# Longer minima and maxima, and other places for GpSimd's turns, in a quantile kernel

## The chip, the core and the metric

The kernel runs on one core of a Trainium2 chip. A core has TensorE (PE, matrix products into PSUM), VectorE (DVE, elementwise work), ScalarE (ACT), GpSimd (POOL) and SyncE (SP), each with its own queue of instructions, and 16 DMA engines. SBUF is the working memory of 128 partitions, PSUM holds matrix products, DRAM the large tensors. The metric is the device time of the whole program in microseconds (us), the median of several runs.

## The reference

There are 4096 nodes with 128 features. A 0/1 matrix `adj` says who is whose neighbour: each entry is 1 with probability 0.0078, so that a node has about 32 neighbours.

Layer 0 is graph attention with 8 heads: for each node a softmax over its neighbours, a weighted sum of their features, two dense products, and a layer norm. Its result is x1, again 4096 x 128.

Layer 1 takes quantiles. For each node the list of its neighbours is thinned (with more than 5 neighbours, every `skip`-th one in the list is left out, where skip is half the number, rounded up). Of the kept neighbours' rows of x1, each of the 128 features is sorted on its own, and the entries at the places of the quantiles 0.25, 0.5 and 0.75 are averaged:

```python
vals = jnp.where(keep[:, :, None], x[None, :, :], big)
svals = jnp.sort(vals, axis=1)
for q in QUANTILES:
    idx = jnp.maximum(jnp.ceil(q * n_keep).astype(jnp.int32) - 1, 0)
    picked = jnp.take_along_axis(svals, idx[:, None, None], axis=1)[:, 0, :]
    agg = agg + w_q * picked
```

The mean is mixed half and half with the node's own row, multiplied by a 128 x 128 matrix, and the own row is added.

## The kernel before

**First part (lines 302 to 494).** The kernel finds each node's neighbours from `adj`, ranks the nodes by the number of neighbours, and handles them 128 at a time, a tile, in that order: one node per partition. For the attention it fetches each neighbour's row by an indirect DMA on GpSimd's queue (`gather`, line 221; one such transfer fetches one neighbour's row for each of 128 nodes). The result x1 goes to DRAM. The lists `idx` for layer 1, and the weights `wt` that pick the quantiles, are made beside it. The change touches nothing of this.

**Second part, the quantile stage (lines 498 to 535).** Nodes are in order of their number of neighbours, so that the nodes of one tile need lists of nearly the same length. A unit is one tile, or two tiles side by side (`UNITS`, line 79): tiles 2 to 23 go in pairs, the others alone, 21 units. Their order is tile 0, tiles 24 to 31, the pairs from 22/23 down to 2/3, and tile 1.

For each unit:
- `fetch_unit` (line 509) gathers the neighbours' rows of x1 into `vals`, one slot of 128 columns for each place of the list and each tile of the unit, and the nodes' own rows into `xs`. That makes 23 to 70 gathers for one unit. `vals` has two buffers, so that a unit is fetched while another is sorted.
- `quantile_out` (line 1166) runs a selection network on VectorE: minima and maxima of slots at a distance d, stage by stage, cut down to those that the wanted places (`targets`) need. Slots that stand in a row, or at a regular step, go as one `tensor_tensor` instruction (line 1223). Results go back and forth between two buffers `work0` and `work1`, and those that are final into `goal`.
- TensorE picks the quantiles out of `goal` by products with diagonal matrices (lines 1239 to 1251), multiplies by the layer's matrix, and ScalarE copies the result `o` out of PSUM (line 1268). `write_out` (line 521) scatters `o` to the output by indirect DMAs on GpSimd's queue.

**The order on GpSimd's queue.** In the loop of lines 527 to 533 the fetch of the next unit is issued first, then the write-out of the unit that was finished before, and then the sort of the present unit goes to VectorE. So while unit k is sorted, GpSimd stands at the write-out of unit k-1, then fetches unit k+2 (into the buffer that unit k has read), then waits for unit k's result.

**Turns.** VectorE's minima and maxima and GpSimd's gathers get in each other's way. The kernel therefore puts a tiny copy from PSUM, `junk<-still` (line 1194, `turn_of_gpsimd`), into VectorE's sequence from time to time. Where it stands is decided while the program is built: `then` (line 1189) adds up an estimate `ran` of the time since the last turn, from the constants `TT_FIX`, `TT_EACH` and `TT_OVER`. Three limits use it:
- if a piece would bring `ran` above `TURN_MAX`, it is cut so that `TURN_AIM` is reached (line 1213), or, where no slot fits any more, a turn is put first (line 1215);
- after each instruction, if `ran` is above `TURN_MIN`, a turn is put (line 1230).

By that estimate 1024 columns after a turn make 0.148 + 1024 x 0.001042 = 1.215, and 2048 columns 2.282.

Of the kernel before, what the change touches and what calls it, by code (L numbers as in the profile page):

```python
# [87 lines left out]


TT_FIX, TT_EACH, TT_OVER = 0.148, 0.001042, 0.077  # L90
TURN_MIN, TURN_AIM, TURN_MAX = 1.25, 1.45, 1.7


R_NUM, R_OWN, R_F1 = L, L + 1, L + 2
# [1401 lines left out]
```

## Time and profile before

| | us |
|---|---|
| median of 3 runs (lowest, highest) | 3682.77 (3679.86, 3687.81) |
| the profiled execution, whole | 4612.32 |
| its span, first to last instruction | 4610.5 |
| first gather of `vals` | 2539.1 after the start of the span |
| VectorE busy from 2680 to 3350 | 647.8 of 670 |
| VectorE busy from 3350 to 4605 | 1047.2 of 1255 |
| GpSimd busy from 3350 to 4605 | 615.8 of 1255 |

The profiled execution is recorded by the hardware's profiler, instruction by instruction, and took 930 us longer than the runs do. Shares and sums in the profile are of that execution. In the profile a group is written as line, engine, operation, what it writes and reads, and its number; behind the bar stand busy time, mean duration in ns, and the idle time of the engine just before, with what ended it. A list in order of time has the start, the duration, and in brackets the idle time before. A GpSimd record of a gather is the making of its descriptors, and not the transfer of the data.

### The profile page before, as it was taken

To read this page: it belongs to the slowest core of one execution; us is meant where nothing else is said; L and a number is where in the kernel's file an instruction comes from. 1 tells how busy PE (TensorE), PEld (TensorE's weight loads), DVE (VectorE), ACT (ScalarE), POOL (GpSimd) and SP (SyncE) were. 2 spreads that over 40 slices of the span, in tenths; PEclk is the share of its full clock that TensorE was granted. 3 is DMA by queue.
4 is the path that set the end of the run, shared out by engine and by line. 5 is a ranking of instruction groups with operands and counts; after the bars stand their busy time and mean duration, and the time that the engine had idled before them with its cause. 6 is when DMAs were issued, how large, how long until landed. Compare 5 with 4: busy or idle time off the path is not lost. (4 is left out here: it accounts for less than half of the span.)

```text
span 4610.5 us, 23017 instructions
## 1 busy us (share of the span) xinstructions
PE 1260.0 (27%) x5372; PEld 961.7 (21%) x5375; DVE 2754.3 (60%) x7608; ACT 399.4 (9%) x555; POOL 2364.5 (51%) x2344
## 2 busy tenths in 40 slices
PE   5264546555243425334245000000000000000001
PEld 2023323333243425324245000000000000000001
DVE  6274446655142212212254289989987977887788
ACT  2020212211011001000001000000000000000000
POOL 1616543243755566464532756677665355565530
PEclk9995556555556555555555555555555555555555
DMA  5321423220211111111110111111111011111100
GB/s 186 92 90 48 141 69 101 96 94 23 61 43 38 43 43 50 36 45 45 45 29 20 50 35 39 41 44 42 41 38 34 24 32 31 36 39 37 36 22 4
DMA packets 109537, 237.71 MB, mean 52 GB/s; under 512 B 47072, under 2 KB 63456, under 8 KB 101200
## 3 DMA queue, kind: packets, MB, share of 16 engines
q0 software_dynamic: 74464, 156.55, 12.2%
q10 hardware_dynamic: 14848, 70.85, 4.5%
q1 hardware_dynamic: 20080, 8.77, 0.8%
q8 instruction: 44, 0.72, 0.1%
q14 instruction: 101, 0.83, 0.1%
HBM read 224.85 MB, written 11.15 MB: 51 GB/s over the span
## 5 line engine op out<-in xcount | busy, mean ns | idle before, releaser
L221 POOL DMA_INDIRECT G<-xt_d,idx x1127 | 1090.3, 967 | 1109.5 <-PE y L1012 696.0
L221 POOL DMA_INDIRECT vals<-x_d,idx x1024 | 1076.9, 1052 | 337.5 <-issue 302.0
L1223 DVE TENSOR_TENSOR work<-work 128x512 f32<-128x512 f32 (+6 forms) x1405 | 960.6, 712 | 35.8 <-remote 22.1
L1223 DVE TENSOR_TENSOR work<-work,work 128x512 f32<-128x512 f32 (+5 forms) x958 | 605.6, 656 | 47.6 <-remote 35.7
L1242 PE MATMUL st_ps<-dg,goal 128*128 128x128 f32 x286 | 71.8, 430 | 1935.4 <-DVE goal L1223 1791.8
L1012 PE MATMUL y<-wide,G 128*128 128x32 f32 (+2 forms) x2254 | 463.1, 381 | 97.3 <-issue 71.6
L1242 PEld LDWEIGHTS st_ps<-dg,goal 128*128 128x128 f32 x286 | 63.9, 325 | 1941.5 <-issue 1940.6
L1012 PEld LDWEIGHTS y<-wide,G 128*128 128x128 f32 x2254 | 443.6, 297 | 120.4 <-issue 86.1
L976 DVE TENSOR_SCALAR rden<-small 4x256 f32<-4x256 f32 x32 | 13.0, 407 | 648.1 <-remote 583.6
L650 DVE MAX8 first<-key 128x8 f32<-128x128 f32 x1024 | 225.5, 282 | 253.6 <-remote 128.7
L230 POOL DMA_INDIRECT out_dram<-o,own_i x32 | 50.8, 1588 | 556.6 <-ACT o L1268 539.2
L1194 DVE COPY junk<-still 128x1 f32<-128x1 f32 x1295 | 194.6, 150 | 206.2 <-remote 97.4
L683 PE MATMUL key<-sgn,markb 128*128 128x512 bf16 x256 | 147.2, 575 | 398.9 <-DVE first L650 171.2
L982 PE MATMUL rz<-rden,ownT 4*128 4x32 f32 (+6 forms) x460 | 113.3, 416 | 515.9 <-DVE rden L977 431.4
L982 PEld LDWEIGHTS rz<-rden,ownT 4*128 4x128 f32 x460 | 101.8, 317 | 532.2 <-issue 364.0
L1031 PE MATMUL hT<-late,W_sb 128*128 128x128 f32 x512 | 112.8, 409 | 238.1 <-issue 160.2
L644 ACT ACTIVATE sgn<-adj_t 128x2048 bf16<-128x2048 int32 x64 | 122.1, 1908 | 557.3 <-PE key L683 273.5
L1223 DVE TENSOR_TENSOR work<-vals 128x1024 f32<-128x1024 f32 (+8 forms) x140 | 138.7, 1007 | 32.7 <-DMA vals<-x_d,idx 32.4
L1031 PEld LDWEIGHTS hT<-late,W_sb 128*128 128x128 f32 x512 | 104.7, 312 | 249.7 <-issue 167.1
L1241 ACT ACTIVATE dg<-ident,wt 128x128 f32<-128x128 f32 x143 | 47.6, 394 | 1191.8 <-PE st_ps L1242 1191.5
L686 PE MATMUL key<-parts,oneb 64*128 64x512 bf16 x256 | 146.5, 572 | 4.8 <-issue 4.6
L1042 PE MATMUL small<-W_sb,late 128*128 128x128 f32 x512 | 120.3, 429 | 33.4 <-DVE late L1039 33.4
(184 smaller groups left out, 1743.0 us busy)
## 6 DMA issues: line engine op xcount, KB each, us to landing
adj_t<-in_adj_dram ACTq DMA_DIRECT2D x64, 1024.0 KB
G<-xt_d,idx POOLq DMA_INDIRECT x1127
vals<-x_d,idx POOLq DMA_INDIRECT x1024
R<-rec_d SPq DMA_DIRECT2D x128, 26.2 KB
xt_d<-rec SPq DMA_DIRECT2D x4, 544.0 KB
rec<-in_x_dram ACTq DMA_DIRECT2D x4, 512.0 KB
narrow<-rec_d SPq DMA_DIRECT2D x72, 5.2 KB
a_b<-in_L_gnn_a_dram ACTq DMA_DIRECT2D x2, 512.0 KB
```

The source lines that it names most:

```text
L221: nc.gpsimd.indirect_dma_start(out=dst, out_offset=None, in_=rows, in_offset=bass.IndirectOffsetOnAxis(ap=idx, axis=0),)
L644: nc.scalar.activation(sgn, adj_t, AF.Sign, accum_out=cnt[:, i : i + 1])
L650: nc.vector.max(first[:, ts(c0 // CW + c, 8)], key[:, ts(c, CW)])
L683: nc.tensor.matmul(key, lhsT=markb, rhs=sgn[:, ts(b, 512)], start=True, stop=False)
L686: nc.tensor.matmul(key, lhsT=oneb[0:64, :], rhs=parts[1][:, ts(r - 1, 512)] if r else parts[0], start=False, stop=True)
L982: nc.tensor.matmul(rz[:, layer[i] * H : (layer[i] + w - g0) * H], lhsT=ownT[w][:, r, :], rhs=rden.rearrange("p (g r h) -> p r g h", r=k // ...
L1012: nc.tensor.matmul(yf[:, ts(g, c)], lhsT=G[:, col + j - a, 0:D], rhs=pf[:, ts(j, c)], start=(i == 0 and g % (w // 2) == w // 2 - 1), stop= ...
L1031: nc.tensor.matmul(hT[:, ts(h, P)], lhsT=consts["W_sb"][:, h, :], rhs=yT[:, h, :], start=True, stop=True)
L1042: nc.tensor.matmul(o, lhsT=hv[:, h, :], rhs=consts["W1_sb"][:, h, :], start=(h == 0), stop=(h == H - 1))
L1194: nc.vector.tensor_copy(junk, late["still"])
L1223: nc.vector.tensor_tensor(slots_of(dst, (j, c, s, m), size), slots_of(a, (i, c, s, m), size), slots_of(b, (i + d, c, s, m), size), op,)
L1242: nc.tensor.matmul(st_ps[:, u, :], lhsT=goal[:, (j * k + u) * D : (j * k + u + 1) * D], rhs=dg, start=(j == 0), stop=False,)
```

## The change

Only the three limits change:

```diff
 TT_FIX, TT_EACH, TT_OVER = 0.148, 0.001042, 0.077
-TURN_MIN, TURN_AIM, TURN_MAX = 1.25, 1.45, 1.7
+TURN_MIN, TURN_AIM, TURN_MAX = 1.1, 1.9, 2.4
```

An instruction of 2048 columns (2.282 by the estimate) is now left whole where it follows a turn; before, it was cut at about 1024 to 1152 columns. An instruction of 1024 columns (1.215) is now followed by a turn at once; before, this was so only where the next piece didn't fit. What is compared with what, and in which order, stays the same, as do all instructions of the other engines.

## The prediction

> **What bounds the kernel now.** I read the page's busy times and slices first, then the groups by line, then the list in order of time around two places, then the busy times by stretch. The page splits the program at about 2540 us. Before it TensorE, GpSimd and VectorE share the attention layer. After it VectorE is busy in seven to nine tenths of every slice and TensorE almost nowhere: the quantile stage, the only one that the change touches.
>
> Groups of the page (busy us, mean ns, then idle before and what ended it):
>
> ```profile
> L221 POOL DMA_INDIRECT vals<-x_d,idx x1024 | 1076.9, 1052 | 337.5 <-issue 302.0
> ...
> L1223 DVE TENSOR_TENSOR work<-work 128x512 f32<-128x512 f32 (+6 forms) x1405 | 960.6, 712 | 35.8 <-remote 22.1
> L1223 DVE TENSOR_TENSOR work<-work,work 128x512 f32<-128x512 f32 (+5 forms) x958 | 605.6, 656 | 47.6 <-remote 35.7
> ...
> L230 POOL DMA_INDIRECT out_dram<-o,own_i x32 | 50.8, 1588 | 556.6 <-ACT o L1268 539.2
> ...
> L1194 DVE COPY junk<-still 128x1 f32<-128x1 f32 x1295 | 194.6, 150 | 206.2 <-remote 97.4
> ```
>
> GpSimd waits 539 us in this stage for a finished unit (the write-out stands in its queue behind the fetch), while VectorE waits for data only at the start. So VectorE bounds the stage and GpSimd has slack. How the two mesh shows in order of time (start, duration, engine):
>
> ```profile
> 3299.07 1.30 POOL L221 DMA_INDIRECT vals<-x_d,idx  x1 [0.30 <-issue]
> 3299.48 0.14 DVE L1194 COPY junk<-still 128x1 f32<-128x1 f32 x1
> 3299.55 1.28 DVE L1223 TENSOR_TENSOR work<-work,work 128x512 f32<-128x512 f32 x2
> 3300.68 0.97 POOL L221 DMA_INDIRECT vals<-x_d,idx  x1 [0.30 <-issue]
> 3300.75 0.14 DVE L1194 COPY junk<-still 128x1 f32<-128x1 f32 x1
> 3300.82 0.41 DVE L1223 TENSOR_TENSOR work<-work,work 128x256 f32<-128x256 f32 x1
> ```
>
> A gather takes 0.94 us when nothing is in its way (most of them do). One that starts during a run of minima and maxima lasts longer by exactly the time to the next turn: 3299.07 + 1.30 - 0.94 = 3299.43, the turn's start. Pairing the trace's lists of both engines: of some 420 lengthened gathers between 2690 and 4560 us, 262 end their wait within 0.05 us of a turn's start; most others end it where VectorE itself stood still. So: one gather per turn, and the turn after it if the gather comes too late. Its own cycle is 0.94 + 0.30 = 1.25 us.
>
> A turn's copy lasts 0.15 us but costs VectorE far less: it starts at 3300.75, and the next maximum at 3300.82. Two 512-column instructions take 1.20 us from start to the turn (3299.55 to 3300.75), 0.600 each; a 1024-column one 1.13 to 1.14. So each instruction costs 1.042 ns per column and 0.067 us, a turn 0.067 us. Summed over a unit this gives the trace: tile 24 counts 65.9 us and took 66.9, tile 31 145.9 and 146.4.
>
> The profile has one more thing, which decides how it stands to the runs. VectorE stands still, at turns above all, when gathers have come back to back for some 30 times, and in the first stage all engines but GpSimd do:
>
> ```profile
> 1640.34 1.87 ACT L1025 COPY late<-y 128x1024 f32<-128x1024 f32 x1 [50.72 <-remote]
> 1689.99 0.41 DVE L976 TENSOR_SCALAR rden<-small 4x256 f32<-4x256 f32 x1 [89.72 <-remote]
> ...
> 3538.07 0.16 DVE L1194 COPY junk<-still 128x1 f32<-128x1 f32 x1 [2.42 <-remote]
> ...
> 3542.28 0.16 DVE L1194 COPY junk<-still 128x1 f32<-128x1 f32 x1 [2.85 <-remote]
> ```
>
> Such slips (over 0.3 us) sum to about 300 us in the quantile stage: 72 in the first unit, 22 in tile 29, 208 in the pairs. The profiled execution took 4612 us, the runs 3683. Had the runs these slips, this stage would take 4612 - 2539 (its first gather) = 2073 us there too and leave 1610 for the first. But the first stage's some 1218 indirect transfers from 112.4 us on need 1218 x 1.247 = 1519, 1631 in all, without any wait. So I take the slips for an effect of the recording, absent from the runs or nearly so.
>
> **What the Trainium skill says.** "SBUF — State Buffer", Who interferes with whom: a VectorE instruction with two SBUF inputs contends with a GpSimd instruction that reads SBUF, and one with at most one SBUF input outside the 2-port modes doesn't. The trace agrees: gathers (they read their indices) wait out tensor_tensor runs and get in at the copy out of PSUM. The page has the loser block fully, which is what the 0.36 us extra shows. "Perfetto Trace Analysis", Optimizing Scalar/DVE Operations: about 60 ns of access overhead per VectorE instruction, profiled latency about twice that. Measured: 67 ns, and 150 ns of recorded length beyond the columns. Same page, GPSIMD Engine Instruction: time GpSimd by start-to-start spacing. I do: 1.25 us.
>
> **The change, part by part.** Columns don't change: 1,382,784 in either program, x 1.0417 ns = 1440.4 us. Evaluating the planning loop with both sets of constants gives 2649 minima/maxima and 1295 turns before, 2250 and 1118 after.
> 1. Fewer cuts: 67 pieces of 2048 columns and 120 of 1536 appear, those of 1024 go from 492 to 358, of 512 from 923 to 666: 399 instructions less x 0.067 = 26.7 us.
> 2. Fewer turns (the lower TURN_MIN adds some, the higher limits remove more): 177 x 0.067 = 11.9 us.
> 3. VectorE's stage is then 1440.4 + 3368 x 0.067 = 1666.1 against 1440.4 + 3944 x 0.067 = 1704.6: 38.6 us less.
> 4. What GpSimd loses. Between turns lie up to 2.3 us instead of 1.7. No instruction moves past another on GpSimd, SP, ACT or TensorE; only the chances to enter go. Behind a waiting gather stand the rest of its fetch, the write-out, and the next fetch. While a pair of tiles is sorted, GpSimd fetches the unit two places later. Tiles 22/23 and 20/21 have 78 turns for 66 gathers. From then on it is short: 59 turns for 62, 59 for 62, 55 for 58, 56 for 58, 50 for 58, 51 for 54, and two write-outs in each. Shortfall with these 34 turns, at 1.6 us each (mean distance) 54 us over the six pairs. It is covered by the lead of one whole unit (a fetch is due only after the following unit, 80 to 95 us).
>
> To see whether the cover lasts I stepped through both orders of instructions with prices from the trace alone: VectorE by item 3, a gather let in at a turn (or up to 0.08 us after it, the latest that the trace shows), 0.94 + 0.305 us each, data 1.9 us after the last gather, the first gather of a unit once the unit two before has read its values, a write-out 6 to 7.5 us after the sort ends. Fed with the trace's own turns, this rule gives the fetches' lengths to within 6 us, most within 2 (tile 26: 51.7 against 51.3). Without slips, before takes 1769 us from first gather to end (43 of it waits for the first two units), after 1731 (45). The last fetches land just 6 us before VectorE needs them (tiles 4/5 and 2/3). So GpSimd's loss costs nothing here, but its cover is almost used up: from there each missed turn costs some 1.6 us.
> 5. Sum: -38 us. Against the profiled 4612 it would be 4574 if the slips stayed; but slower gathers (1.5 to 1.6 us in pairs, where tiles 24 to 28 at 1.4 had none) should also remove most of the pairs' 208 us, so that I expect a profiled execution of 4350 to 4570. Against the runs: 3682.8 - 38 = 3645.
>
> The unknown in 1 is a 2048-column instruction, which the trace lacks: by the line through 512 and 1024 columns 2.28 us long. Were it 5% slower, 67 x 0.11 = 7 us; faster than the line there is no reason.
>
> **Rivals.**
> GpSimd becomes the bound, and the kernel slower. Place: the pairs 10/11 to 2/3. A gather must be ready at the turn after the one that it used; behind 1024 columns that turn comes after 1.20 us, the gather's cycle is 1.247. The trace has VectorE held 0.045 us by the gather that enters just then, which keeps the two in step. It decides where the cycle exceeds about 1.26 us, or the window is narrower: then turns are missed. With that rule the count gives 27 us slower than before (some misses) to 80 (step lost everywhere, before being slower itself too): 3710 to 3763. For it: 6 us of margin. Against: 142 gathers in the trace enter 0.07 us behind a turn, in step; a random 0.05 us delay in 3% of the gathers costs only 2 us.
> The slips are real in the runs. Then slower gathers save part of 300 us too: 3683 - 38 - 50 to 190, 3455 to 3595. Against: the sum above.
> The gain isn't there: the 0.067 us is hidden by something else, or GpSimd's misses eat it: 3675 to 3690. Against: units without slips take what the count says.
>
> **How the numbers follow.** Gain as counted 0.53 (3630 to 3660); slips real 0.07; no difference 0.08; GpSimd the bound 0.32, for which the margin of 6 us and an untried pattern of turns speak. A difference under 0.2% (7 us) is about what can't be told from none. Likeliest 3645, its own range 3630 to 3660. For 8 in 10 the range goes down to 3610 (the slips' case left out) and up to 3750 (the worst of GpSimd's left out). Faster 0.60, same 0.08, slower 0.32.
>
> **What would show it.** 1118 turns of 0.15 us; 67 instructions of 128x2048 at about 2.28 us; columns' cost unchanged; unit of tile 24 at 64.8 us instead of 66.9; waits of VectorE for vals only in the first two units. Wrong if VectorE waits for vals in the pairs, if GpSimd no longer waits for o, or if 2048 columns cost more than the line.

## The result, and the profile after

| | before | after |
|---|---|---|
| median of 6 runs each, us | 3684.21 | 3649.70 |
| lowest and highest, us | 3679.86, 3692.78 | 3640.43, 3654.08 |
| ratio after/before, 95% interval | | 0.9889 [0.9874, 0.9905] |
| a profiled execution, whole, us | 3687.72 | 3651.08 |
| its span, us | 3685.9 | 3649.3 |

By the medians the kernel became 34.5 us faster, 0.9%; the ratio of the third row stands for 1.1%, or 35 to 46 us by its interval. The forecast was 3645 us. Before takes about 3690 us on the first kind of chip met here and about 4590 on a second kind, and the profile shown ahead of the prediction (4612 us) is like the latter; so it was profiled again on the first kind, which gives the last two rows of its column and the comparison below.

The groups of the page of after (busy us, mean ns, then idle before and what ended it), which answer to those that the prediction showed of before:

```profile
L221 POOL DMA_INDIRECT vals<-x_d,idx x1024 | 1221.7, 1193 | 315.7 <-issue 302.3
...
L1223 DVE TENSOR_TENSOR work<-work 128x512 f32<-128x512 f32 (+7 forms) x1194 | 932.5, 809 | 0.6
L1223 DVE TENSOR_TENSOR work<-work,work 128x512 f32<-128x512 f32 (+6 forms) x821 | 589.3, 738 | 0.5
L1194 DVE COPY junk<-still 128x1 f32<-128x1 f32 x1118 | 166.1, 149 | 0.0
```

The same groups of before, in the profile taken again (the run called e0 below):

```profile
L221 POOL DMA_INDIRECT vals<-x_d,idx x1024 | 1052.5, 1028 | 337.5 <-issue 299.5
...
L1223 DVE TENSOR_TENSOR work<-work 128x512 f32<-128x512 f32 (+6 forms) x1405 | 958.7, 709 | 0.4
...
L1223 DVE TENSOR_TENSOR work<-work,work 128x512 f32<-128x512 f32 (+5 forms) x958 | 604.1, 653 | 0.7
...
L1194 DVE COPY junk<-still 128x1 f32<-128x1 f32 x1295 | 189.6, 146 | 0.0
```

Two things are to be seen. The counts are those that the prediction worked out (1118 turns), and the idle time ahead of minima, maxima and turns, which was 36, 48 and 206 us in the first profile, is under 1 us in both of these. And GpSimd's gathers became longer, 1193 ns against 1028: they wait longer to get in.

The new sizes, from the groups of after with the shapes kept apart:

```profile
L1223 DVE TENSOR_TENSOR work<-work 128x2048 f32<-128x2048 f32 x45 | 102.6, 2285 | 0.0
L1223 DVE TENSOR_TENSOR work<-work 128x1536 f32<-128x1536 f32 x57 | 99.5, 1747 | 0.1
L1223 DVE TENSOR_TENSOR work<-work,work 128x2048 f32<-128x2048 f32 x14 | 32.0, 2291 | 0.0
```

2048 columns take 2285 ns, 1024 take 1224: the second thousand costs 1.036 ns per column, so nothing is lost on these long instructions.

How a gather meets a long maximum, in order of time in unit 6/7 of after (start, duration, engine; idle before in brackets; twelve lines of the other engines are left out):

```profile
3387.48 1.75 DVE L1223 TENSOR_TENSOR work<-vals 128x1536 f32<-128x1536 f32 x1
...
3388.61 1.43 POOL L221 DMA_INDIRECT vals<-x_d,idx  x1 [0.30 <-issue]
...
3389.15 0.15 DVE L1194 COPY junk<-still 128x1 f32<-128x1 f32 x1
3389.26 2.29 DVE L1223 TENSOR_TENSOR work<-work 128x2048 f32<-128x2048 f32 x1
...
3390.35 2.02 POOL L221 DMA_INDIRECT vals<-x_d,idx  x1 [0.31 <-issue]
3391.47 0.15 DVE L1194 COPY junk<-still 128x1 f32<-128x1 f32 x1
```

The gather of 3390.35 would be done at 3391.29; it waits for the turn at 3391.47 and ends 0.90 us behind that. VectorE runs on without a pause: it is GpSimd that pays for the long instruction.

Where the 34.5 us came from. In the two profiles on this kind of chip the time from the first minimum of the quantile stage to the last is 1739.3 us before (1932.9 to 3672.2) and 1699.4 after (1936.2 to 3635.6): 39.9 less. The first stage was 3.3 us longer in after's profile, which the change can't have caused (with the same first part, the first gather of `vals` comes at 1891 to 1913 us in the profiles of e5 and e6 below). Seven of the 21 units, each from its first minimum to the next unit's:

| unit | us before | us after | instructions and turns saved | each x 0.067 |
|---|---|---|---|---|
| tile 24 | 66.9 | 65.1 | 30 | 2.0 |
| tile 31 | 146.4 | 144.3 | 33 | 2.2 |
| 22/23 | 115.6 | 113.0 | 34 | 2.3 |
| 18/19 | 98.5 | 94.2 | 42 | 2.8 |
| 10/11 | 82.8 | 79.9 | 35 | 2.3 |
| 6/7 | 84.5 | 81.6 | 35 | 2.3 |
| 2/3 | 64.4 | 63.3 | 25 | 1.7 |

The gains are of the size that the instructions saved give, though single units differ by up to 1.5 us. 18/19 shows what else is in them: before has 1.9 us there that the count of columns and instructions doesn't explain, and after 0.4. In before, 58 of its turns have a gather starting within 0.12 us of them, and these 58 start 1.5 us later in sum than the count gives; in after there are 25 such turns, with 0.2 us. So a small part of the gain seems to come from gathers that arrive less often just at a turn. Over all units what is beyond the count falls from 20.4 to 17.3 us. With the 38.6 us of the count, and the second unit's wait (below) longer by 1.6, this makes 40.1 us, against 39.9 measured.

The waits of both engines in the quantile stage of after, behind the first unit (us in total, times, longest), and below them GpSimd's in before, profiled again:

```profile
DVE work L1223 <- DMA vals<-x_d,idx: 15.6, 1, 15.6
POOL out_dram L230 <- ACT o L1268: 81.9, 5, 31.4
```

```profile
POOL out_dram L230 <- ACT o L1268: 277.1, 14, 59.1
```

VectorE waits once, at the start of the second unit (14.0 us in before), and 32.4 us for the first unit in either kernel. GpSimd's slack, its wait for a finished unit, fell from 277 to 82 us. Of the 5 waits left, 3 (24 us) come before 2900 us and 2 (58 us) after 3575, where nothing is left to fetch; through the later pairs GpSimd never waits for a unit.

How much cover is left can be read more directly. The lead of a fetch, from the end of its last gather of `vals` to the first minimum of that unit, worked out from the lists of both engines:

| unit | before, us | after, us |
|---|---|---|
| 22/23 | 114.7 | 92.2 |
| 18/19 | 139.4 | 115.1 |
| 14/15 | 107.1 | 79.6 |
| 10/11 | 95.0 | 54.0 |
| 8/9 | 86.1 | 37.1 |
| 6/7 | 80.0 | 19.8 |
| 4/5 | 87.2 | 10.9 |
| 2/3 | 86.4 | 11.3 |

In before the lead settles at 80 to 87 us, where a fetch can't begin earlier, because the write-out ahead of it and its buffer hold it. In after it melts from pair to pair, and at the end 11 us are left, of which the data take 1.6 to 2 (what lies between the last gather and the first minimum where VectorE waits for it).

### The profile page after: what moved, and what is told of

Its sections match the earlier page's. It is cut to its first block, busy times and chain, and to the rows that moved or that the text cites. A ratio compares the mean times of both kernels' runs of the same rounds, so it can differ in the third digit from the quotient of the medians.

```text
span 3649.3 us, 22393 instructions
## 1 busy us (share of the span) xinstructions
PE 1233.9 (34%) x5375; PEld 940.8 (26%) x5375; DVE 2702.5 (74%) x7032; ACT 397.5 (11%) x555; POOL 2538.0 (70%) x2344
## 5 line engine op out<-in xcount | busy, mean ns | idle before, releaser
L221 POOL DMA_INDIRECT G<-xt_d,idx x1127 | 1121.7, 995 | 498.5 <-issue 325.3
L221 POOL DMA_INDIRECT vals<-x_d,idx x1024 | 1221.7, 1193 | 315.7 <-issue 302.3
L1223 DVE TENSOR_TENSOR work<-work 128x512 f32<-128x512 f32 (+7 forms) x1194 | 932.5, 809 | 0.6
L1223 DVE TENSOR_TENSOR work<-work,work 128x512 f32<-128x512 f32 (+6 forms) x821 | 589.3, 738 | 0.5
L1012 PEld LDWEIGHTS y<-wide,G 128*128 128x128 f32 x2254 | 427.6, 290 | 48.7 <-DVE wide L999 27.3
L951 DVE TENSOR_TENSOR z<-G,f1x 128x128 f32<-128x128 f32 (+5 forms) x93 | 29.2, 326 | 433.5 <-DMA G<-xt_d,idx 431.9
L1223 DVE TENSOR_TENSOR work<-vals 128x1536 f32<-128x1536 f32 (+7 forms) x96 | 133.3, 1402 | 48.4 <-DMA vals<-x_d,idx 48.0
L966 PE MATMUL small<-z,own 128*4 128x32 f32 (+6 forms) x460 | 49.1, 272 | 351.6 <-ACT z L958 351.6
L1194 DVE COPY junk<-still 128x1 f32<-128x1 f32 x1118 | 166.1, 149 | 0.0
L966 PEld LDWEIGHTS small<-z,own 128*4 128x4 f32 x460 | 27.0, 100 | 370.6 <-ACT z L958 356.9
```

The lines of the kernel that those rows point to most:

```text
L221: nc.gpsimd.indirect_dma_start(out=dst, out_offset=None, in_=rows, in_offset=bass.IndirectOffsetOnAxis(ap=idx, axis=0),)
L1012: nc.tensor.matmul(yf[:, ts(g, c)], lhsT=G[:, col + j - a, 0:D], rhs=pf[:, ts(j, c)], start=(i == 0 and g % (w // 2) == w // 2 - 1), stop= ...
L1194: nc.vector.tensor_copy(junk, late["still"])
L1223: nc.vector.tensor_tensor(slots_of(dst, (j, c, s, m), size), slots_of(a, (i, c, s, m), size), slots_of(b, (i + d, c, s, m), size), op,)
```

## The experiments

Theory A is the prediction's: VectorE bounds the stage by instructions at 0.067 us each, and GpSimd's fewer chances cost nothing as long as a fetch leads. The rivals: GpSimd has become the bound or is within a hair of it (B); the stalls of the first profile are real and the change acts on them (C). Two smaller questions ride along: what makes a turn a turn, and which of the three limits does what. Nothing is left out of the computation in any of the kernels; two of them fetch more than is used. The ratios are each to before on the same chip.

### Is the first profile's standstill an effect of the recording?

e0 is before, unchanged, profiled once more.

> The kernel before, profiled once more. If the standstills of VectorE (300 us in the quantile stage) and of the other engines (first stage) belong to the disturbed execution that was profiled first, a span of about 3682 us, no slip of VectorE over 0.3 us but for the start of the second unit, and a quantile stage of 1769 us from its first gather to the end. If they belong to the kernel before, they show again, with 2073 us in that stage.

Measured: 3687.72 us with the recording, while the runs without it on the same chip have a median of 3690.18. No pause of over 0.3 us lies inside any unit. So recording cost nothing that could be measured. On two other chips before takes 4587.11 and 4593.49 us as the median of runs that aren't recorded, with a granted TensorE clock (0.57) like that of the first chip (0.574 in the median). So the standstills of the first profile belong to the chip, or to the condition that it is in, and not to the recording. They are not in the quantile stage alone: of the 925 us between the two profiles, 635 lie ahead of the first gather of `vals`. What sets such a chip apart wasn't found.

### How near is GpSimd to being the bound?

Three more gathers per unit, 63 in all, into a tile that nobody reads: e5 adds them to after, e6 to before.

```diff
+            for _ in range(3):
+                more = fp.tile([P, D], F32, name="more", bufs=2)
+                gather(nc, more, x1_d, own_i[:, unit[0] : unit[0] + 1])
```

> The kernel after with three gathers more for each unit, into a tile that nobody reads (63 in all). Theory (GpSimd's cover is used up but for 6 us): each unit's fetch is late by three turns from the pairs on, 60 us slower than after, 3710, waits of VectorE for vals of some 105 us. Rival (GpSimd has slack as before): within 5 us of after.

> The kernel before with the same three gathers more for each unit. Theory (before has a surplus of turns): 3 to 6 us slower than before, 3688. If GpSimd bound it already: 63 x 1.25 = 79 us slower.

Measured on the chip with before at 3690.18:

| | us | ratio to before |
|---|---|---|
| e5, after with 3 more | 3693.86 | 1.0007 [0.9999, 1.0016] |
| e6, before with 3 more | 3693.61 | 1.0009 [0.9998, 1.0020] |

The same extra work costs before 3 us, which can't be told from none, and after some 44 (against the 3649.70 of its own runs; 43.5 by the two ratios to before), which is more than the whole gain. Waits in the quantile stage of e5, then of e6:

```profile
DVE work L1226 <- DMA vals<-x_d,idx: 58.1, 6, 19.3
DVE work L1226 <- issue: 3.0, 1, 3.0
POOL out_dram L230 <- ACT o L1271: 39.0, 2, 25.5
```

```profile
DVE work L1226 <- DMA vals<-x_d,idx: 18.9, 1, 18.9
POOL out_dram L230 <- ACT o L1271: 187.7, 10, 59.6
```

In e5 VectorE waits for `vals` in the pairs, 61.1 - 19.3 = 41.8 us beside the wait of the second unit. In the units: 8/9, 6/7 and 4/5 last 90.3, 95.3 and 85.2 us where after has 81.6, 81.6 and 76.4, and 3 to 4 us more pass before the next one begins. The last gather of 8/9 ends 8.8 us after that unit's first minimum, that of 6/7 13.8 after. In e6 the lead is still about 80 us or more in every pair. So after is at the edge: VectorE bounds it, with a margin of 9 us (11 less the data's 2) on GpSimd's side at the end of the pairs, which six more gathers at 1.6 us in all would use up by this estimate. Theory B's mechanism is real, and in after it is just not reached.

### Which limit does what?

```diff
-TURN_MIN, TURN_AIM, TURN_MAX = 1.1, 1.9, 2.4
+TURN_MIN, TURN_AIM, TURN_MAX = 1.25, 1.9, 2.4     # e1, e8: longer pieces alone, 2271 minima/maxima, 971 turns
+TURN_MIN, TURN_AIM, TURN_MAX = 1.1, 1.45, 1.7     # e2, e9: earlier turns alone, 2582 minima/maxima, 1318 turns
```

> Only TURN_AIM and TURN_MAX as in the kernel after (1.9, 2.4), TURN_MIN stays 1.25. The plan has 2271 minima/maxima and 971 turns (before 2649 and 1295, after 2250 and 1118). Theory (one gather per turn, GpSimd's loss is hidden only as long as turns suffice): VectorE has 702 instructions less to issue, 47 us at 0.067, but the pairs have 41 to 64 turns for 54 to 66 gathers, so GpSimd becomes the bound: about 78 us slower than before, 3745 to 3780, with waits of VectorE for vals of some 180 us in the quantile stage. Rival (GpSimd doesn't bind, VectorE's instruction count alone decides): 47 us faster than before, 3637.

> Only TURN_MIN as in the kernel after (1.1), TURN_AIM and TURN_MAX stay 1.45 and 1.7. 2582 minima/maxima and 1318 turns. Theory: 44 instructions less x 0.067 = 3 us, less a little lost to gathers: 1 to 3 us faster than before, which can't be told from no change, 3678 to 3685. Rival (the turn behind each 1024 columns is what gives the gain): 30 us or more faster.

These went to a chip of the other kind, and were repeated there as e8 and e9 (on a third chip):

> As e1 (TURN_MIN 1.25, TURN_AIM 1.9, TURN_MAX 2.4), wanted on a chip on which the kernel before takes its 3684 us and VectorE doesn't stand still. One gather per turn: 971 turns, 41 to 64 for the 54 to 66 gathers of a pair, GpSimd becomes the bound, 78 us slower than before, ratio 1.02, waits of VectorE for vals of some 180 us. Rival, VectorE's count of instructions alone: 47 us faster, ratio 0.987.

> As e2 (TURN_MIN 1.1, TURN_AIM 1.45, TURN_MAX 1.7), for the same reason. 44 instructions less: 1 to 3 us faster than before, ratio 0.999 to 1.000. Rival, the turn behind each 1024 columns gives the gain: ratio 0.99.

| | us | before there | ratio |
|---|---|---|---|
| e1, longer pieces | 4372.68 | 4587.11 | 0.9537 [0.9500, 0.9575] |
| e8, the same | 4376.47 | 4593.49 | 0.9521 [0.9476, 0.9566] |
| e2, earlier turns | 4634.49 | 4587.11 | 1.0102 [1.0069, 1.0136] |
| e9, the same | 4634.46 | 4593.49 | 1.0083 [1.0045, 1.0122] |

The forecasts for e1 and e2 (slower by some 78 us, and no change) were made for the first kind of chip; neither came true here. On this kind of chip the standstills decide. The waits of VectorE in e2, from 2500 us on:

```profile
DVE junk L1194 <- remote: 127.8, 50, 4.2
DVE work L1223 <- remote: 56.0, 14, 8.1
```

And a stretch of e2's tile 24 in order of time, where VectorE loses 2.1 us ahead of a turn while gathers follow each other:

```profile
2698.60 1.00 POOL L221 DMA_INDIRECT vals<-x_d,idx  x1 [0.30 <-issue]
2699.91 0.94 POOL L221 DMA_INDIRECT vals<-x_d,idx  x1 [0.30 <-issue]
2700.93 0.16 DVE L1194 COPY junk<-still 128x1 f32<-128x1 f32 x1 [2.14 <-DVE work L1223]
```

Summed over the units (starts that come over 0.3 us later than the count gives): the first profile of before has 302 us, 208 of it in the pairs; e2 has 352, of which 27 are in tiles 24 to 26 where before has none, and 39 in tile 29 instead of 22. That is 50 us more, and less 3 for the 44 instructions and turns saved the 47 us by which e2 is slower. That this agrees to a microsecond is luck: the interval of e2's ratio is 31 us wide. Earlier turns let gathers come closer to one another, at 1.25 us where nothing holds them up. In e1 the pairs have no standstill but for late data; there each gather waits for a turn of a longer rhythm:

```profile
3641.88 2.27 DVE L1223 TENSOR_TENSOR work<-work 128x2048 f32<-128x2048 f32 x1
3643.01 1.96 POOL L221 DMA_INDIRECT vals<-x_d,idx  x1 [0.30 <-issue]
3644.07 0.14 DVE L1194 COPY junk<-still 128x1 f32<-128x1 f32 x1
...
3645.28 1.96 POOL L221 DMA_INDIRECT vals<-x_d,idx  x1 [0.30 <-issue]
```

One gather in 2.27 us. That it is the slower gathers, and not something else in e1, that take the standstills away is argued from these traces; no run changed the gathers' rhythm alone. And e1 pays for it as theory B has it, and as after doesn't on its chip (waits of VectorE in e1 from 3300 us on, all in the pairs):

```profile
DVE work L1223 <- DMA vals<-x_d,idx: 31.8, 4, 13.7
DVE work L1223 <- issue: 13.8, 2, 9.4
```

45.6 us, in 8/9, 6/7 and 4/5 and between them and the next: with 43 or 44 turns in each of 10/11, 8/9 and 6/7 where after has 50 and 51, GpSimd falls behind. The balance of e1 is then: standstills in the pairs -208 and in tile 29 +5; 3944 - 3242 = 702 instructions less, -47; waits +46; together -204, against -214 measured, in part luck again.

What this says of the change on the first kind of chip, where there are no standstills: the longer pieces should bring the gain (by the count 3242 instructions and turns, 8 us less than after even), and the earlier turns, which cost 8 us, should keep GpSimd from falling behind. An estimate from e1's waits: 3650 - 8 + 46 = 3688, no gain. It may be too low: in e1 the first unit stands still for some 70 us while GpSimd fetches on, so that tile 24's fetch leads by 58.6 us, where in after, on the first kind of chip, it leads by 1.7. Neither limit ran alone on the first kind of chip, so this division is argued and not shown, and the forecast of +78 us for e1 there stays untested.

e4 and e10 set the limits by unit, less work where the lead is long and more turns where gathers come close:

```diff
+OTHER = {
+    0: (1.2, 1.45, 1.7), 24: (1.2, 1.45, 2.4), 25: (1.2, 1.45, 2.4), 26: (1.2, 1.45, 2.4),
+    29: (1.2, 1.45, 2.4), 30: (1.4, 1.45, 2.8), 31: (1.2, 1.45, 4.0),
+    22: (1.1, 2.1, 2.4), 20: (1.1, 2.1, 2.4), 18: (1.1, 2.1, 2.4), 16: (1.1, 2.1, 2.4),
+    4: (1.1, 2.1, 2.4), 2: (1.7, 1.45, 4.0), 1: (2.5, 2.1, 4.0),
+}
...
+    least, aim, most = OTHER.get(unit[0], (TURN_MIN, TURN_AIM, TURN_MAX))
... (and these three in place of the constants in the loop)
```

> The kernel after with other limits for some units, chosen so that each unit has little more turns than the gathers need: 2238 minima/maxima and 1072 turns. By the count 7 us faster than after, 3643, at the edge of what can be measured; if turns can't be spared even there, slower than after.

> As e4 (limits by unit, 2238 minima/maxima, 1072 turns), for the same reason. 7 us faster than after, ratio to before 0.987.

Measured: 4361.54 (0.9491 [0.9456, 0.9527]) and 4352.82 (0.9485 [0.9443, 0.9528]), the least of what ran on these chips, by 11 and 24 us below e1 and e8, though their single runs overlap. By the count (2238 and 1072) it would be 4 us of instructions below after on the first kind of chip, and not the 7 of the expectation; it didn't run there, and after didn't run on these, so whether it beats after is open.

### What a turn costs, and what makes it one

e3 does the turn's copy twice:

```diff
         nc.vector.tensor_copy(junk, late["still"])
+        nc.vector.tensor_copy(junk, late["still"])
```

> The kernel after with the copy of each turn issued twice, 1118 copies more. If a turn costs VectorE 0.067 us, 64 to 75 us slower than after (the lower end because a longer turn spares the small delays by which gathers and VectorE keep step), 3714 to 3725. If the recorded 0.15 us were its cost: 166 us slower. If GpSimd were the bound and VectorE had slack: under 20 us slower.

Measured: 4587.73, ratio 0.9989 [0.9968, 1.0010], on a chip of the second kind, where after wasn't measured, so the total says nothing of the price. The trace does. In tile 24 of e3 (start, duration):

```profile
2702.37 0.15 DVE L1194 COPY junk<-still 128x1 f32<-128x1 f32 x1
2702.55 0.16 DVE L1195 COPY junk<-still 128x1 f32<-128x1 f32 x1
2702.63 0.42 DVE L1224 TENSOR_TENSOR work<-work,work 128x256 f32<-128x256 f32 x1
```

The second copy, which writes what the first wrote, comes 0.18 us behind it, and its record has it wait for VectorE's own semaphore; the minimum, which doesn't depend on it, comes 0.08 us behind the second. So this was a poor yardstick: two copies on one tile aren't two independent turns. Tile 24 lasted 73.4 us in e3, 8.3 more than in after for 46 turns, which is 0.18 each. The price of 0.067 holds for an instruction that waits for nothing.

e7 makes the turn a minimum of one column with two inputs from SBUF instead of a copy out of PSUM, e11 one of 128 columns:

```diff
-        nc.vector.tensor_copy(junk, late["still"])
+        nc.vector.tensor_tensor(junk, late["ones"][:, 0:1], late["ones"][:, 0:1], ALU.min)    # e7
+        nc.vector.tensor_tensor(junk, late["ones"], late["ones"], ALU.min)                    # e11, junk 128 wide
```

> The kernel after with the turn's copy from PSUM replaced by a minimum of one column with two SBUF inputs; nothing else changes, the value isn't used. If the port must be free of two-input instructions (theory), gathers get in only while VectorE waits: fetch and sort follow one another, about 1290 us longer than after, some 4900. If it is enough that one long instruction ends and another begins, the same time as after, 3650.

> The kernel after with each turn replaced by a minimum of 128 columns with two SBUF inputs, whose value isn't used: 1118 x 128 / 960 = 149 us more for VectorE. If a turn works because it is one more end and start in VectorE's sequence, whatever its length, about 3650 + 149 = 3800 us or less. If it must be short, gathers get in only where VectorE waits, and the time is 1290 us longer on top, some 5000.

e7 took 3651.61 us in its one run, the same as after. Its order of time:

```profile
2302.24 1.30 POOL L221 DMA_INDIRECT vals<-x_d,idx  x1 [0.31 <-issue]
2302.64 0.15 DVE L1194 TENSOR_TENSOR junk<-ones 128x1 f32<-128x1 f32 x1
2302.71 1.28 DVE L1223 TENSOR_TENSOR work<-work 128x512 f32<-128x512 f32 x2
2303.84 0.97 POOL L221 DMA_INDIRECT vals<-x_d,idx  x1 [0.30 <-issue]
```

2302.24 + 1.30 - 0.94 = 2302.60: the gather got in at this turn as it does at the copy out of PSUM. Of the gathers that had to wait 563 got in at such a turn, and none passed one. So the prediction's reading, that the turn lets GpSimd in because it has at most one input in SBUF, falls; what lets it in is not the operands' place.

e11 took 4510.84 us in its one run, on the second kind of chip. A turn costs 0.20 us there, as the price says for 128 columns (128 x 0.00104 + 0.067), and tile 24 takes 71.2 us, 6.1 more than in after: 46 x 0.133. Most of its gathers, some 750 of 860 that had to wait, still got in at a turn, though these last 0.28 us. But not all: four write-outs lasted 24 to 28 us and three gathers 6, 11 and 95 us, where in the other kernels no gather or write-out lasted over 3.7. The longest:

```profile
3281.35 95.49 POOL L221 DMA_INDIRECT vals<-x_d,idx  x1 [0.30 <-issue]
```

61 turns and 165 minima and maxima start while it lasts. The fetch of 20/21 came late by it, and the lead didn't come back: VectorE waited for `vals` again in the pairs 14/15 to 4/5. So a turn needn't be a copy from PSUM, but one of 128 columns is less sure to let a gather in than one of a single column; why isn't known.

An ordinary boundary between two minima lets a gather in, too. Of the gathers that had to wait, by where the wait ended (within 0.1 us), 310 in before (e0) got in at a turn and 70 at an ordinary boundary; in after 522 and 12. That the ordinary boundaries are few is because few gathers meet one first. In before a gather stood waiting at 74 ordinary boundaries and got in at 70 of them, in e1 at 49 of 50, but in after at only 12 of 42; the 30 missed ones belong to 11 gathers. At a turn of one column none was missed, in before or in after. Dependence alone doesn't decide it: of the 30 missed boundaries 10 begin an instruction that waits for VectorE's own semaphore, and 20 one that doesn't. So the turns are the surer way in, and not the only one. No kernel without turns ran, so how many of them are needed at all is open.

## Why the prediction was right, point by point

- **Steps 1 to 3, the instructions.** Right in count, price and sum. 1118 turns, 67 of 128x2048 (59 with inputs in `work` alone, 8 with inputs in `vals`); 0.067 us per instruction saved holds for the sum; in the seven units listed it comes to 0.044 to 0.10, the rest being small delays as in 18/19. The figure of about 60 ns that the prediction set beside it (the Trainium skill, "Perfetto Trace Analysis", Optimizing Scalar/DVE Operations) is for operands in SBUF; the same sentence has about 125 ns for PSUM, from which a turn copies, and the trace shows 0.07 us from a turn to the next start for either (after and e7). Said: the stage 38.6 us shorter from first minimum on; measured 39.9. Said: from the first gather to the end of the sort 1769 before and 1731 after; measured 1768.4 and 1728.5. Tile 24 was to last 64.8 us and lasted 65.1.
- **The unknown, 2048 columns.** Taken at 2.28 us, measured 2.28 to 2.29. The allowance of 7 us for a slower one wasn't needed.
- **Step 4, GpSimd.** Right: VectorE waits for `vals` only in the first two units. The counted margin was 6 us; measured 11 from the end of the last gather, 9 when the data's 1.9 us are taken off. That more work for GpSimd costs from there on was confirmed with three gathers per unit; their price was set too high, at 60 us, and was 44. Which part of the count overshot wasn't separated. One part of the rule was too narrow: that a gather gets in at turns alone, and that most of the others that waited in the first profile ended it where VectorE stood still. By the trace 73 of those got in at ordinary boundaries. It did little harm, as in after 522 of 534 got in at turns.
- **Step 5, the sum, and how the profile stands to the runs.** The number came out: -38 said, -34.5 measured. The reason given was wrong in one step. "I take the slips for an effect of the recording": e0 was recorded without any, and runs that weren't recorded have them on other chips. The argument from the first stage (1631 us needed without a wait) was sound as far as it went: it showed that the runs of 3683 us had no slips, not why. Nor did the forecast of a profiled execution at 4350 to 4570 us come true (3651), as it presumed that the next recording would carry them too.
- **The rivals.** GpSimd as the bound (0.32) didn't come; e5 shows that it was near and what it would have looked like: VectorE waiting for `vals` in the last pairs. Slips real in the runs (0.07): not on the chip that was measured; where they are real, those of the pairs are gone with fewer and longer pieces (e1: all of 208 us), which fits the forecast's "slower gathers (1.5 to 1.6 us in pairs, where tiles 24 to 28 at 1.4 had none) should also remove most of the pairs' 208 us".
- **The Trainium skill's rule on ports** ("SBUF — State Buffer", Who interferes with whom). That a gather waits out minima and maxima is seen in every trace here. That the turn works because of its PSUM operand is not: e7. A wait mostly ends with the one instruction that runs (70 of 74 ordinary boundaries in e0), and not only with the next turn, as the prediction read it.

## What to carry to other kernels

Price a tiny instruction that is put in or taken out by what it moves the start of the next one (0.067 us here), not by its recorded length (0.15), and see first whether its neighbour depends on it (0.18). When an edit takes away chances of the other engine, count per unit what it needs against what it gets, and follow the lead of each fetch to the end of the stage: a gain can be whole while the lead melts from 86 to 11 us, and a few added transfers in both kernels show how close the edge is. When a profile's execution and the runs differ by a quarter, profile again before reasoning on its stalls.

## What the runs showed of the hardware that was not expected

- One program takes 3690 us on one chip and 4587 or 4593 on two others. There, VectorE stands still for up to 8 us at a time. In the pairs of the first profile the first standstill comes after 29 to 37 gathers of a fetch at 1.25 to 1.28 us on average; in those of e1, where the fetches run at 1.55 to 1.81 us on average, there is none but the waits for late data.
- The way for a gather past a run of two-input minima isn't opened by a copy from PSUM in particular: a one-column minimum with two SBUF inputs does as well (3651.6 against 3649.7 us), and an ordinary boundary between two minima mostly does (70 of 74 in e0, 12 of 42 in after). A minimum of 128 columns does less surely: one gather passed 61 of them (e11).
- A copy right behind another that writes the same column starts 0.18 us after it, against 0.07 to 0.08 for an instruction that doesn't wait for it.
